# Two transformer layers on one core: layer 1's fill, tables and tail in another order

## The chip, the cores and the metric

The kernel runs on one core of one Trainium2 chip. The metric is the device time of one execution in microseconds; the time of a kernel is the median of its runs. Every number of the profile comes from one further execution, taken by the hardware profiler.

## The reference

Two layers work on x of shape (8, 256, 128), 8 batches of 256 tokens. Each layer first makes six vectors per batch from a condition, then an attention step and a feed-forward step. Cut to what matters:

```python
sa, ca, ga, sb, cb, gb = split6(silu(c) @ wmod)     # ga, gb kept at |.| >= 0.25
h = layernorm(x) * (1 + ca) + sa
x = x + ga * attention(h)                           # causal; layer 0: 16 heads of 8, layer 1: 16 heads of 64
h = layernorm(x) * (1 + cb) + sb
x = x + gb * ffn(h)
# ffn of layer 0: a shared gelu MLP, and top 2 of 8 experts
# ffn of layer 1: h + shared MLP + top 2 of 16 experts, by a sigmoid router;
#                 an MLP is (silu(h @ wg) * (h @ wu)) @ wd with 64 hidden values
```

All values are float32.

## The kernel before, in words

**Tiles and order.** Tokens stand 128 to a tile; four tiles, two batches, are a block of 512 columns, and there are four blocks (NW = 4, LAST = 3). The order of instructions is written by hand: each engine executes what is issued to it in program order, and it waits where an operand or a buffer isn't ready. Buffers come from pools; a tile takes a slot of its tag, and waits for the tile that had it before, so two uses of one tag with two slots can wait for each other. In PSUM the tags are `s` (two slots of two banks: scores, projections' hidden products `gu`, `gud`, `gus`), `o` and `sum` (one each), and `p` (two slots: what `ps_ln` hands out, the norm's transposes `nt1b`, the turned rows `xT`, the router's logits, the output product `y`).

**Layer 1's attention** runs over 32 units n (b, u = divmod(n, 4): batch and four heads). In unit n PE makes the scores of n (L1670), projects queries and keys for n+2 (L1639), values for n−1 (L1692, the output `o`; L1700, the sums) and projects values for n+2 (L1652); ACT takes exponentials (L1673), POOL masks the causal half (L822), DVE copies `o` out (L1704). Around each unit lists of further steps are hung in: `at(n)` before the values, `at_end(n)` after the unit, `at_head(n, k)` behind the k-th piece of scores. When the four units of a batch are done, `reciprocals1` (L1708 to L1716) takes the reciprocal of the sums, writes it to DRAM (`rd`) and reads it back spread over partitions (`rb`); `normalise1` (L1725) multiplies with it on DVE, and `finish1` (L1745 to L1752) is the output product on PE and the addition to x. For the last batch `spread_last` (L1733, L1737) spreads the reciprocals by a product on PE instead.

**Layer 1's feed-forward step, batches 0 to 5** (blocks 0 to 2) is sorted by expert. `norm1` makes the norm of a span of batches: `xn1b` (L766 on DVE), its transposes and h, the tokens `ht` (L1768, L1769 on POOL), and `add_h` (L1773, L1774 on POOL), which adds gb·h to x. `route1` (L1794 to L1820) picks the two experts and scatters the tokens into sorted rows `xs` in DRAM by indirect DMAs of POOL (L932). Before the first scatter `xs` is filled with zeros by `clear` (L889, one DMA of 12,582,912 bytes on SP's queue, issued at the end of unit 8). Then ten groups of four tiles of sorted rows are worked off: groups 0 to 3 are the first tiles of the 16 experts, in known places (`fetch_rows1`, L1830); groups 4 to 9 are the tiles that are needed beyond those, and which expert and which rows these are stands in two small tables, `rowi` and `widx`. `tables_steps` (L957 to L1004) makes them from the counts of tokens: a product on PE (L963) and 14 operations on DVE. SP reads the tables into registers, for the weights in `fetch_weights1` (L1850, L1854) and for the rows in `find_rows1`, and then loads with them (`load_rows`, L1046). Per group: `turn1` turns the rows (PE L1869, copied by ACT, L1871) and orders the rows of the group four further on, `hidden1` makes the two hidden products (PE L1880, silu on ACT L1885, multiplication on DVE L1886), `project_tiles` projects down (PE L1893) into two PSUM tiles, both copied by DVE (L1899) and stored (`ys`, L1900). When all is stored, 24 indirect DMAs of POOL (`gather1`, L1058) fetch each token's two rows, and `combine1` (PE L2018) adds them with weights, by products with diagonal matrices that `weigh1` makes on ACT (L2010).

**Batches 6 and 7** (block 3, LAST) are done densely, over all 16 experts, two at a time: `dense_hidden(p)` for p = 0 to 7 (PE L1942, silu on ACT L1936, multiplication on DVE L1937), `dense_gate(p)` (DVE L1947, the multiplication with the router's gates, which `gate_rows`, L1917 to L1927, spreads over partitions through DRAM) and `dense_project(p)` (PE L1952). `shared_hidden` and `shared_project` (L1962, L1976) are the shared MLP, and `ffn1_add` (L1988 to L1994) the last addition and the store of a block. The order of the tail stands as a plain list of calls at the end of the function.

**Layer 0** is in the change with one step: `gates0`, four small DVE operations (L1255 to L1259) that pick the gates, hung into an attention unit.

## Time and profile before

| what | us |
|---|---|
| runs of the kernel | 573.43, 575.76, 576.96 (median 575.76) |
| the profiled execution | 605.03 |
| its span (first to last instruction) | 603.2 |
| PE busy in the span | 543.5 (90%) |
| DVE busy | 323.8 (54%) |
| ACT busy | 265.5 (44%) |
| POOL busy | 265.2 (44%) |

The span begins at 0. A line of the timeline gives the start, the time from the first to the last of the instructions merged in it, engine, line of the kernel, operation, output and input tiles, their shapes, and how many instructions it holds; in brackets stand the idle time of the engine before it and what ended that. `PEld` is the loading of weights into PE, `SPq` the queue on which SP issues its DMAs. Where the releaser is "issue" or "remote", the trace shows nothing that the engine waited for. A line of the windows gives a stretch's start and end, its length, and each engine's busy time in it with the number of instructions; `PEclk` is the share of PE's full clock that was granted, 0.965 over the whole span.

### The profile page before, as it was taken

How to read it: one execution, taken by the hardware profiler on the slowest of the kernel's cores; microseconds unless marked ns; L12 is line 12 of the kernel's file. 1: busy time of each engine (PE TensorE's matmuls, PEld its weight loads, DVE VectorE, ACT ScalarE, POOL GpSimd, SP SyncE). 2: the span in 40 equal slices, each digit the busy share in tenths (PEclk: the TensorE clock that was granted, in tenths of full speed). 3: DMA queues.
4: the chain of work that ended last, by engine and by line, in shares of the span. 5: the costliest groups of instructions: out<-in, count | busy, mean ns of one | idle time of the engine just before them, and what ended most of it. 6: DMA issues, size and time to landing. Idle time of an engine off the chain costs nothing.

```text
span 603.2 us, 12004 instructions
## 1 busy us (share of the span) xinstructions
PE 543.5 (90%) x4499; PEld 384.4 (64%) x4499; DVE 323.8 (54%) x988; ACT 265.5 (44%) x495; POOL 265.2 (44%) x404
## 2 busy tenths in 40 slices
PE   5999998889999998999999989999999989885194
PEld 4355554468999986666767666766767677742064
DVE  4258886666422224655366646558374757771143
ACT  3678775244556633653344423462534322262010
POOL 5224576574444123855123525333563440647400
PEclk9999999799999999999999999999999999987688
DMA  8699100315999713104069831203030355555101
GB/s 278 243 399 406 56 19 27 129 44 155 327 342 354 238 39 153 36 18 99 1 211 408 326 72 46 60 3 71 14 93 10 82 175 170 166 148 131 36 19 57
DMA packets 53566, 85.40 MB, mean 142 GB/s; under 512 B 6652, under 2 KB 32764, under 8 KB 52348
## 3 DMA queue, kind: packets, MB, share of 16 engines
q1 hardware_dynamic: 45308, 60.50, 31.3%
q0 software_dynamic: 8048, 23.67, 12.1%
q8 instruction: 37, 0.61, 0.4%
q10 hardware_dynamic: 144, 0.39, 0.2%
q14 instruction: 29, 0.24, 0.1%
HBM read 53.46 MB, written 31.07 MB: 140 GB/s over the span
## 4 chain that ended last, share of the span: by engine, by line
PE 68%; DVE 12%; DMA 6%; ACT 5%; issue 3%; another core or an unknown queue 3%; SPq 1%; POOL 0%; DVEq 0%; ACTq 0%; POOLq 0%
PE sc L1670 6%; PE hp L1351 6%; PE yt L1359 6%; PE sc L1120 5%; PE o L1692 5%; PE qp L1639 5%; PE y L1745 5%; PE kp L1639 4%; PE vp L1652 4%; PE o L1154 3%; PE sum L1700 3%; DMA rb<-rd 2%; PE gud L1942 2%; DVE ou L1725 2%
## 5 line engine op out<-in xcount | busy, mean ns | idle before, releaser
L822 POOL TENSOR_SCALAR_AFFINE_SELECT pt<-pt 128x256 f32<-128x256 f32 (+1 forms) x144 | 67.1, 494 | 153.8 <-ACT pt L1673 118.3
L1058 POOL DMA_INDIRECT yg<-ys,yidx x56 | 53.9, 963 | 40.7 <-issue 20.5
L1673 ACT ACTIVATE pt<-sc 128x768 f32<-128x768 f32 x64 | 48.4, 808 | 31.2 <-PE sc L1670 31.1
L1136 ACT ACTIVATE pt<-sc 128x1024 f32<-128x1024 f32 x48 | 46.7, 1026 | 24.6 <-PE sc L1120 11.7
L1670 PEld LDWEIGHTS sc<-q,k 64*128 64x128 f32 x512 | 41.6, 187 | 18.7 <-issue 13.8
L1670 PE MATMUL sc<-q,k 64*128 64x256 f32 (+1 forms) x512 | 50.5, 337 | 0.0
L1353 ACT ACTIVATE hst<-hp,wt 128x128 f32<-128x128 f32 x136 | 38.8, 368 | 25.8 <-ACT hst L1353 24.2
L1692 PE MATMUL o<-pt,v 128*64 128x256 f32 (+1 forms) x512 | 48.7, 332 | 1.2 <-DVE ou L1704 1.2
L1655 ACT COPY v<-vp 128x512 f32<-128x512 f32 x32 | 18.7, 585 | 67.4 <-PE vp L1652 67.4
L1050 POOL DMA_INDIRECT wt<-in_wpk_dram,widx x31 | 29.5, 950 | 34.0 <-PE xT L1342 28.3
L1692 PEld LDWEIGHTS o<-pt,v 128*64 128x64 f32 x512 | 31.8, 136 | 18.2 <-issue 5.0
L1643 DVE COPY q<-qp 128x512 f32<-128x512 f32 x32 | 22.0, 688 | 37.3 <-PE qp L1639 37.3
L1364 DVE COPY ysb<-yt 128x128 f32<-128x128 f32 x39 | 11.3, 290 | 49.8 <-PE yt L1359 49.8
L1639 PE MATMUL qp<-h,wq 128*128 128x256 f32 x128 | 36.1, 404 | 1.7 <-DVE sh L1309 1.3
L1120 PE MATMUL sc<-qm,k 32*128 32x512 f32 x192 | 36.0, 722 | 1.4 <-ACT pt L1136 0.8
L1745 PE MATMUL y<-wo,ou 128*128 128x128 f32 x256 | 31.7, 281 | 5.9 <-DVE ou L1725 3.0
L932 POOL DMA_INDIRECT xs<-ht0b,idx x32 | 31.9, 998 | 11.2 <-issue 7.7
L1745 PEld LDWEIGHTS y<-wo,ou 128*128 128x128 f32 x256 | 29.9, 192 | 9.9 <-DVE at L922 4.6
L1652 PE MATMUL vp<-wv,h 128*128 128x512 f32 x64 | 36.0, 645 | 0.0
L1351 PE MATMUL hp<-xTs,wt 128*128 128x128 f32 x272 | 35.9, 275 | 0.0
L1359 PE MATMUL yt<-wt,hst 128*128 128x128 f32 x272 | 35.8, 275 | 0.0
L1351 PEld LDWEIGHTS hp<-xTs,wt 128*128 128x128 f32 x272 | 33.0, 192 | 0.0
(308 smaller groups left out, 1080.9 us busy)
## 6 DMA issues: line engine op xcount, KB each, us to landing
xs<-zero SPq DMA_DIRECT2D x1, 12288.0 KB
xs<-zero SPq DMA_DIRECT2D x1, 8192.0 KB
rb<-rd SPq DMA_DIRECT2D x14, 512.0 KB
mdb<-mrd SPq DMA_DIRECT2D x2, 2048.0 KB
xg<-xs SPq DMA_DIRECT2D x63, 64.0 KB
wt<-in_wpk_dram SPq DMA_DIRECT2D x24, 128.0 KB
wst<-in_wpk_dram SPq DMA_DIRECT2D x5, 514.0 KB
ys<-ysb SPq DMA_DIRECT2D x10, 256.0 KB
```

The source lines that it names most:

```text
L822: nc.gpsimd.affine_select(out=pt, in_=pt, compare_op=ALU.is_ge, fill=0.0, base=0, pattern=[[0, pt.shape[1]], [1, P]], channel_multiplier=-1,)
L1058: nc.gpsimd.indirect_dma_start(out=yg[:, k, :], out_offset=None, in_=self.ys[:, :], in_offset=bass.IndirectOffsetOnAxis(ap=self.yidx[:, j, ...
L1120: nc.tensor.matmul(out=sc[:, n, :].rearrange("p (a q) -> p a q", q=rhs.shape[2]), lhsT=k[r, cols], rhs=rhs, start=True, stop=u < 2,)
L1136: nc.scalar.activation(pt[:, bass.ts(half, 2), :], sc, AF.Exp)
L1351: nc.tensor.matmul(out=hp[:, c, :], lhsT=wt[:, bass.ts(c, P)], rhs=xT, start=True, stop=True)
L1359: nc.tensor.matmul(out=y, lhsT=hs[:, c, :], rhs=wt[:, bass.ds(WF + c * P, P)], start=(c == 0), stop=(c == FC - 1))
L1639: nc.tensor.matmul(out=ps_[:, n, :], lhsT=w1[f"w{what}1"][:, bass.ts(2 * u + n, P)], rhs=hb, start=True, stop=True)
L1652: nc.tensor.matmul(out=vp, lhsT=hb[:, bass.ts(j, P)], rhs=w1["wv1"][:, bass.ts(half, 512)], start=True, stop=True)
L1670: nc.tensor.matmul(out=sc[:, n, cols], lhsT=k[r, m, bass.ts(kb, P)], rhs=q[r, m, qs], start=True, stop=True)
L1673: nc.scalar.activation(pt, sc[:, :, 0:384], AF.Exp, scale=1.0 / math.sqrt(D1))
L1692: nc.tensor.matmul(out=o[bass.ts(n, D1), m, qs], lhsT=v[:, kb, bass.ts(4 * (u % 2) + 2 * m + n, D1)], rhs=pts[m][:, n, cols], start=(kb == ...
L1745: nc.tensor.matmul(out=y[:, j, :], lhsT=aT[:, c % 2, c // 2, bass.ts(j, P)], rhs=w1["wo1"][:, c, :], start=(c == 0), stop=(c == NC1 - 1),)
```

## The change

1. The fill of layer 1's `xs` is split into three DMAs of a third each, at the ends of units 4, 8 and 12, each behind the issues of that batch's reciprocals. The scatters wait for all three.
2. Layer 0's third step of the first gates goes from the end of unit 20 to the end of unit 21.
3. `spread_last` takes its PSUM tile from `ps_ln` (tag `p`) in place of tag `s`.
4. Of `project_tiles`' two copies out of PSUM the second goes from DVE to ACT.
5. `add_h` of the spans (2, 2) and (4, 1) comes one unit later (end of unit 23 and 27 in place of 22 and 26).
6. The first step of the tables and the weights of groups 4 and 5 go from the end of unit 29 to the end of unit 31, the tables ahead of what is done there already; the rows of groups 0 to 3 stay at unit 30 and so come ahead of the weights on SP's queue; the reading of the row table and the weights of group 6 go to the end of unit 31.
7. In the tail combines 0 to 3 go ahead of the dense gates, and hidden products, gates and dense products alternate: hidden(n), gate(n−2), product(n−2).

```diff
-        def clear(self, zero):
+        def clear(self, zero, part=0, parts=1):
             m = zero.shape[1]
-            self.fill = nc.sync.dma_start(
-                out=self.xs.rearrange("(p a) c -> p (a c)", p=P).rearrange("p (n m) -> p n m", m=m),
-                in_=zero.unsqueeze(1).to_broadcast([P, self.ne * self.cap // m, m]),
-            ).ins
+            n = self.ne * self.cap // m // parts
+            rows = self.xs.rearrange("(p a) c -> p (a c)", p=P).rearrange("p (n m) -> p n m", m=m)
+            self.fills.append(
+                nc.sync.dma_start(
+                    out=rows[:, bass.ts(part, n), :], in_=zero.unsqueeze(1).to_broadcast([P, n, m])
+                ).ins
+            )
...
-                tc.add_manual_dep(ins, self.fill.name, WAIT, reason="rows are cleared first")
+                for fill in self.fills:
+                    tc.add_manual_dep(ins, fill.name, WAIT, reason="rows are cleared first")
...
-    at_end(20, first_gates)
+    at_end(21, first_gates)
...
-            rp = pp.tile([P, 2, S], F32, tag="s", name=f"rp1_{u}")
+            rp = ps_ln([P, 2, S], f"rp1_{u}")
...
-        for k in range(2):
-            nc.vector.tensor_copy(ysb[:, :, k, :], y[k])
+        nc.vector.tensor_copy(ysb[:, :, 0, :], y[0])
+        nc.scalar.copy(ysb[:, :, 1, :], y[1])
...
-            at_end(n + 4 if bs[0] else n + 7, add)
+            at_end(n + 5 if bs[0] else n + 7, add)
     tables = one(z1.tables_steps(ps_ln, True))
-    at_end(29, tables, lambda: fetch_weights1(4), lambda: fetch_weights1(5))
-    at_end(30, *[lambda m=m: fetch_rows1(m) for m in range(4)], *[lambda m=m: find_rows1(m) for m in range(4, NQ)],
-          lambda: fetch_weights1(6))
+    at_end(30, *[lambda m=m: fetch_rows1(m) for m in range(4)])
+    ends[N - 1].insert(0, tables)
+    at_end(
+        N - 1, lambda: fetch_weights1(4), lambda: fetch_weights1(5),
+        *[lambda m=m: find_rows1(m) for m in range(4, NQ)], lambda: fetch_weights1(6),
+    )
...
-            if b == 2:
-                z1.clear(zero1)
+            if b < 4:
+                z1.clear(zero1, b - 1, 3)
...
     dense_hidden(2)
     dense_hidden(3)
+    combine1(0, 1, 2, 3)
     dense_gate(0)
-    dense_hidden(4)
     dense_gate(1)
-    dense_hidden(5)
-    dense_gate(2)
-    combine1(0, 1, 2, 3)
-    ffn1_add(0)
-    dense_hidden(6)
-    dense_gate(3)
     dense_project(0)
     dense_project(1)
+    dense_hidden(4)
+    dense_gate(2)
+    ffn1_add(0)
+    dense_project(2)
+    dense_hidden(5)
+    dense_gate(3)
+    dense_project(3)
+    dense_hidden(6)
+    dense_gate(4)
+    dense_project(4)
     dense_hidden(7)
-    dense_gate(4)
-    combine1(4)
-    dense_project(2)
     dense_gate(5)
-    dense_project(3)
-    combine1(5)
+    dense_project(5)
+    combine1(4, 5)
     dense_gate(6)
-    dense_project(4)
+    dense_project(6)
     combine1(6, 7)
     dense_gate(7)
     ffn1_add(1)
-    dense_project(5)
-    combine1(8)
-    dense_project(6)
-    combine1(9)
     dense_project(7)
-    combine1(10, 11)
     ffn1_add(LAST)
+    combine1(8, 9, 10, 11)
     ffn1_add(2)
```

More of the change, by code (lines that the diff above doesn't have):

```diff
@@ L867, in __init__ @@
             self.placed = 0
-            self.scatters = []
+            self.fills, self.scatters = [], []
             f32 = lambda shape, name: pool.tile(shape, F32, name=f"{name}{tag}")
```

## The prediction, made before the changed kernel had run

> **What bounds the kernel now.** I read the time in stretches first, to see which engine is full where, then the order of instructions around each place the diff touches. The windows (start and length, then each engine's busy time, the granted clock, the DMA share):

> ```profile
> core 0: us, PE busy (x) PEld busy (x) DVE busy (x) ACT busy (x) POOL busy (x), PEclk, DMA share, GB/s
> 300.00:400.00 100.00, 96.67 (x817) 67.69 (x814) 58.04 (x153) 42.12 (x60) 40.47 (x66) 1.00 0.51 170
> 540.00:560.00 20.00, 12.64 (x36) 5.40 (x34) 4.07 (x13) 3.52 (x10) 15.12 (x17) 0.76 0.62 136
> 560.00:575.00 15.00, 2.86 (x4) 1.30 (x5) 1.89 (x3) 1.08 (x2) 4.86 (x6) 0.61 0.11 28
> 575.00:603.00 28.00, 19.49 (x126) 15.34 (x124) 12.53 (x21) 2.39 (x4) 0.00 (x0) 0.87 0.11 40
> ```

> In layer 1's attention PE is busy 97 of 100 us: there only PE's own waits can be won. From 540 on it is not full, so there the order decides. The timeline of the end:

> ```profile
> 570.77 1.08 ACT L1936 ACTIVATE a<-gud 128x512 f32<-128x512 f32 x2 [14.93 <-remote]
> ...
> 581.03 1.02 PE L1942 MATMUL gud<-h,wu 128*128 128x512 f32 x2
> 582.09 0.60 ACT L1936 ACTIVATE a<-gud 128x512 f32<-128x512 f32 x1 [2.91 <-PE gud L1942]
> 582.72 0.69 DVE L1937 TENSOR_TENSOR a<-a,gud 128x512 f32<-128x512 f32 x1 [0.89 <-ACT a L1936]
> 583.32 0.68 DVE L1947 TENSOR_TENSOR a<-a,gp 128x512 f32<-128x512 f32 x1
> ```

> ACT stood 14.93 us before a silu whose input was ready, and 8.41 us before an earlier one (546.84 to 555.25), together 23.3 us, with no releaser in the trace. The profiled execution took 605.03 us (span 603.2) and the median of the runs is 575.76, 29.3 less. The attention is full of PE work and can't give 27 us back; if those two waits are away, PE's work from 542.5 is 8 hidden of 1.72 (13.8), one shared product 1.0, 8 dense products of 0.9 (7.3) and 12 combines of 0.44 (5.3), 27.4 us, to 570, and add and store bring the span to about 574.6, which with the 1.83 us around the span is 576.4. So I read the two waits as the profiled execution's own, and make every sum as a difference on its rows, carried over to 575.76. The 24 gathers (1.25 us apart from 536.60, last landing 567.9) would end at 572.1: PE's tail leads by only 2.5 us.

> **The change, part by part.** *Fill.* Now it is one 12.6 MB DMA from 306.63 to about 344.8. Behind it, the reciprocals' write of batch 2 takes 6.1 us (338.91 to 345.0), where the same write takes 1.7 at 303.72 and at 472.21; the broadcast lands at 352.46, and PE waits:

> ```profile
> 352.48 2.50 DVE L1725 TENSOR_TENSOR ou<-ou,rb 128x512 f32<-128x512 f32 x4 [5.06 <-DMA rb<-rd]
> 353.32 2.87 PE L1745 MATMUL y<-wo,ou 128*128 128x128 f32 x20 [2.25 <-DVE ou L1725]
> ```

> In thirds (10.3 us each, a batch apart, each behind the next broadcast) the write is 4.4 us earlier, and 1.9 of the 2.25 go (1.0 to 2.2): **−1.9**. The last third ends near 358, and the first scatter was at 360.31 and may be 2 earlier: POOL may wait up to 1.5, in front of the causal masks, which have 3 us of cover (they cost 1 if that is gone). The two added issues of 0.5 on SP lie between loads that nobody waits for: 0.

> *Added h a unit later.* DVE's four normalisations take 2.50 alone and 4.72 beside POOL's two additions, and at the second place (449.20) 3.99:

> ```profile
> 415.10 4.72 DVE L1725 TENSOR_TENSOR ou<-ou,rb 128x512 f32<-128x512 f32 x4
> 415.12 1.28 POOL L1773 TENSOR_TENSOR xn1b<-ht,mdb 128x512 f32<-128x512 f32 x1
> 416.47 1.60 POOL L1774 TENSOR_TENSOR x<-x,xn1b 128x512 f32<-128x512 f32 x1
> ...
> 420.01 3.84 PE L1745 MATMUL y<-wo,ou 128*128 128x128 f32 x32 [1.25 <-DVE at L922]
> ```

> PE waits 1.25 there and 1.70 at 453.35; about 2.4 of these 2.95 go. But one unit later the additions meet the normalisation L766 (two of 345 ns, at 429.75 and 463.16), and PE's transposes stand behind it, everything else of PE behind them. The nearest row is L766 beside a POOL operation at 249.84: 994 ns instead of 345, so 0.65 for one operation, about 0.9 a place with the second. [...] I take the row: **−0.6** (−2.4 to 0).

> *Layer 0's gates* (four DVE operations, 0.8 us) leave a place where PE waits 0.99 (103.02) and are put where it waits 0.38 (105.91): **0**. The clock is at half from 103.17 to 113.41 after a window 52% busy; if that is avoided, up to −3; if DVE is late at the new place, +0.5.

> *Tables, weights, rows.* SP's queue, in order of time:

> ```profile
> 484.97 5.38 SPq L1854 DMA_DIRECT2D wt<-in_wpk_dram  x8
> 490.66 2.05 SPq L1830 DMA_DIRECT2D xg<-xs  x4
> 495.37 1.96 SPq L1854 DMA_DIRECT2D wt<-in_wpk_dram  x4
> 497.58 6.75 SPq L1046 DMA_DIRECT2D xg<-xs  x12
> ```

> Today the table's 14 DVE operations (479.31 to 484.42) hold up a copy for which PE waits 1.15 at 485.17. That wait goes. But the table now waits for unit 31's work: its count can run at 486.4, and 4.85 us on, at 491.5, SP may read the indices. Then on SP, in order, 8 weight issues (0.52 each and one pause, 5.4 as above), seven register loads (2.35) and 4 more (2.0), 9.8 to 10.0; only then the four pieces of group 4's rows, issued 501.6 to 503.2 (before: to 499.45), landing 505 to 506 by the 2.5 they take now. The rows of groups 0 to 3 come earlier than before, and nobody waits for them. PE transposes group 4 at 501.34, ending 502.33; it would be at that place at 500.2 and wait 5, ending at about 505.9: **+3.6** (+2.5 to +5; behind it on PE stand hidden1(3) and all that follows, and nothing else is free to run). The clock: [...] it fell after windows 52% (99.75 to 103.17) and 56% busy (529.83 to 533.25), and not after one of 49% (523.01 to 526.42). [...] By the rows it falls for 3.4 us or more: cost up to 2. I take **+1.0**. Weights of groups 4 to 6 are loaded 6 to 7 us later and are wanted after their rows: covered while the rows are the later.

> *Reciprocals' spread in other buffers.* It leaves the pair shared with the hidden products (a wait of 1.31 at 513.44) for the pair of the norm's transposes, which then wait for DVE's multiplication of 0.7: **0** (−0.5 to +0.5).

> *Copies on two engines.* The tail where it matters:

> ```profile
> 531.08 4.79 ACT L2010 ACTIVATE dg<-ident,g 128x128 f32<-128x128 f32 x16
> 531.16 0.41 DVE L1899 COPY ysb<-yq_sum 128x256 f32<-128x256 f32 x1
> 531.29 0.49 PE L1893 MATMUL yq_o<-wt,aq 64*128 64x128 f32 x2 [1.25 <-DVE ysb L1899]
> ```

> Each of ten groups has 0.41 less on DVE, and ACT pays 0.38 each (its silu of the same shape). PE waits for these copies only in groups 7 to 9: about −0.6. But in ACT's program order eight diagonals (half of 4.79, 2.4) stand ahead of group 8's copy, which so ends at 533.4; PE's last group, which needs that buffer, ends at 534.1 instead of 532.3, the gathers start 1.45 later, and the first shared silu at 538.3 instead of 537.18. Net **+0.8** (0.3 to 1.5).

> *Dense products by turns.* In the new order PE does hidden(n), then the product n−2, which needs gate n−2. On DVE gate n−2 stands behind the multiplication of n, that behind the silu of n, and that behind hidden(n) itself. So after each of n = 4, 5, 6, 7 PE has nothing between the end of hidden(n) and the end of that gate. From the rows at 581: hidden ends 582.05, silu 582.09 to 582.69, multiplication to 583.41, gate to 584.00: 2.0 us. Before, products and combines of older groups lay in this gap. 4 × 2.0 = **+8.0**. Gate 0, moved ahead, may wait for the gates' spread: **+0.5** (0 to 1.5). At the end combines 8 to 11 lie beside the last additions: **−0.5**.

> Sum: −1.9 − 0.6 + 0 + 3.6 + 1.0 + 0 + 0.8 + 8.0 + 0.5 − 0.5 = **+10.9**. On the profiled execution as it stands 605.03 would become 616; on the median 575.76 it is **586.7 us**.

> **The rivals.** *The waits of ACT are real in every run, or the gathers hide the turns.* Then combines 0 to 3 and products 0 and 1 (3.7 us of PE work), which now stand ahead of hidden(4), fall into the wait, and the gathers' own chain hides part of the turns: the last stretch costs +2.5 instead of +8.0, and the time is 581. For it: the trace does show the waits. Against it: 27 us fit nowhere else. *The clock falls in the turns.* A turn is 1.72 + 0.98 of work in 4.7, 57% busy, like the windows after which it fell; at half clock over two of the four turns, 2 × 2.7 more: 592; over all of them 597. *Faster:* one mechanism, the place of PE in the trace when group 4's rows land. If these land by 502 (SP not waiting for the table, say 4 us earlier than I have it), the 3.6 and 1.0 are a gain of 1.15, and without that hole the clock keeps up in the tail; with the turns inside ACT's waits (0) and the clock at 103 whole (−3), the sum is −1.9 − 0.6 − 1.15 − 3 = −6.7: 569. It decides at a landing before 502.3. Against it, the table can't start before unit 31's sums. *Nothing:* the gains in the attention and losses behind it cancel, 576; it needs the turns to cost under 3.

> **How the numbers follow.** A difference of 1% (5.8 us) is about what a measurement of this kernel can tell. Forecast 586.7: 0.42; turns half hidden, 581: 0.17; clock falls, 592 to 597: 0.14; nothing, 573 to 579: 0.12; faster, 569: 0.15. The third of these lies wholly above 1%, the first nearly so, of the second a third lies within: slower 0.66, same 0.18, faster 0.16. The range 570 to 596 leaves out the faster half of the last case and the far end of the clock's.

> **What would show it.** Right: no wait of PE at the output product of batch 2; L1725 all near 0.63 us, and L766 slower once or twice; a wait of 4 to 5 us at group 4's transposes, put down to the row's DMA; group 9's products waiting for ACT's copy; and four gaps of 2 us of PE, each ahead of a dense product, with DVE's gate as releaser. Wrong: rows of group 4 there before PE, gaps under 1 us, or ACT's long waits again in the unprofiled time.

## The result, and the profile after

The changed kernel takes 592.35 us (median of 587.9 to 596.18, four runs), the kernel before 574.6 (571.46 to 576.96): 1.031 times as long, 95% interval 1.022 to 1.040. Run once more beside its parts (experiment 5) it took 593.53 against 575.8, 1.034 (1.027 to 1.041). So it is slower by some 18 us, in the stated range; the forecast of 586.7 had +10.9. The profile after is that of the longest of the four runs: 596.18, 593.0, 591.7 and 587.9 us went with mean granted clocks of 0.966, 0.971, 0.973 and 0.975.

On the chip of experiments 1 to 4 the kernel before itself takes 605.64 us (43 runs), and ACT's long waits in the tail are there in every trace (the longest 12.82 to 17.76 us); on the two chips of 5 to 8 and of 9 to 12 it takes 575.8 and 574.96, and they are in none. So each kernel is compared by its ratio to before on its own chip. The ratios of experiments 5 to 8 stand against the 38 of before's 59 runs there that lie below 576.08 us (median 574.21); by the medians of all runs they are 1.0308, 0.9939, 1.0033 and 1.0009.

The windows of the tail after, with the columns as before (start and end, length, busy time of each engine, clock, DMA share, GB/s):

```profile
540.00:560.00 20.00, 15.89 (x72) 9.01 (x70) 7.55 (x18) 5.20 (x13) 15.22 (x16) 0.91 0.63 135
560.00:575.00 15.00, 10.73 (x34) 5.37 (x35) 4.07 (x7) 1.19 (x2) 4.77 (x5) 0.76 0.16 44
575.00:594.50 19.50, 9.27 (x60) 6.98 (x58) 6.69 (x12) 0.60 (x1) 0.00 (x0) 0.76 0.12 44
```

Behind 560 no engine is near full, PE included, and the clock is at 0.76. One turn of the new order in the timeline (lines have moved by 4: L1946 is the hidden product, L1940 the silu, L1941 the multiplication, L1951 the gate, L1956 the dense product):

```profile
567.82 1.87 PE L1946 MATMUL gud<-h,wg 128*128 128x512 f32 x2
569.49 1.91 PE L1946 MATMUL gud<-h,wu 128*128 128x512 f32 x2
571.44 0.60 ACT L1940 ACTIVATE a<-gud 128x512 f32<-128x512 f32 x1 [5.99 <-PE gud L1946]
572.07 0.69 DVE L1941 TENSOR_TENSOR a<-a,gud 128x512 f32<-128x512 f32 x1 [5.30 <-ACT a L1940]
572.67 0.68 DVE L1951 TENSOR_TENSOR a<-a,gp 128x512 f32<-128x512 f32 x1
573.41 1.16 PE L1956 MATMUL of<-wd,a 128*128 128x128 f32 x8 [2.01 <-DVE a L1951]
```

The chain is the one forecast: hidden, silu, multiplication, gate, and PE idle for 2.01 us until the gate is done. It is there four times (560.25, 566.83, 573.41, 579.76), 2.01 each. But the hidden product takes 3.6 us (567.82 to 571.40) where it took 1.9 in the profile before (580.17 to 582.05): a turn lasts 6.58, not 4.7. The windows of PE's clock, cut where the clock changes, show at which clock it ran:

```profile
550.79:554.20 3.41, 1.46 (x13) 1.00 0.85 172
554.20:557.61 3.41, 3.41 (x9) 0.50 0.25 61
557.61:561.02 3.41, 1.40 (x8) 1.00 0.22 60
561.02:564.44 3.42, 3.42 (x8) 0.50 0.45 129
564.44:567.85 3.41, 1.40 (x10) 1.00 0.18 46
567.85:571.26 3.41, 3.41 (x6) 0.50 0.00 0
571.26:574.68 3.42, 1.41 (x10) 1.00 0.00 0
```

In these rows each stretch of 3.41 us with a gap in it has PE busy for 1.40 to 1.46, 41 to 43%, and the next is granted 0.50; there PE is busy for 3.41, the clock of the one behind it is 1.00, and the next gap lies in that. The turn at this mixture of clocks, 6.58, is nearly two stretches (6.83), and the two alternate from 550.79 to 578.09.

Group 4's rows and the copies, in the timeline after:

```profile
483.16 2.05 SPq L1834 DMA_DIRECT2D xg<-xs  x4
487.08 8.92 SPq L1858 DMA_DIRECT2D wt<-in_wpk_dram  x12
496.25 6.12 SPq L1050 DMA_DIRECT2D xg<-xs  x12
...
498.42 1.20 PE L1873 MATMUL xT<-ident,xg 128*128 128x128 f32 x3 [4.59 <-DMA xg<-xs]
...
531.18 0.58 PE L1897 MATMUL yq_sum<-wt,aq 64*128 64x128 f32 x1 [2.43 <-ACT ysb L1903]
```

PE waits 4.59 us for the rows of group 4, and 2.43 for ACT's copy ahead of group 9, both as forecast. And the new place of the added h:

```profile
422.75 1.27 POOL L1777 TENSOR_TENSOR xn1b<-ht,mdb 128x512 f32<-128x512 f32 x1
422.90 2.55 DVE L766 TENSOR_SCALAR xn1b<-x,mv1b,rstd1b 128x128 f32<-128x128 f32 x2
424.10 1.26 POOL L1778 TENSOR_TENSOR x<-x,xn1b 128x512 f32<-128x512 f32 x1
425.50 0.33 PE L775 MATMUL nt1b<-ident,xn1b 128*128 128x128 f32 x1 [0.94 <-DVE xn1b L766]
```

Two operations of DVE, 0.60 us together in the profile before, take 2.55 beside POOL's two.

### The profile page after: what moved, and what is told of

Read it like the earlier page. It is cut to its first block, busy times and chain, and to the rows that moved or that the text cites. A ratio compares the mean times of both kernels' runs of the same rounds, so it can differ in the third digit from the quotient of the medians.

```text
span 594.5 us, 12006 instructions
## 1 busy us (share of the span) xinstructions
PE 544.1 (92%) x4499; PEld 383.2 (64%) x4499; DVE 322.1 (54%) x978; ACT 269.3 (45%) x505; POOL 264.2 (44%) x404
## 5 line engine op out<-in xcount | busy, mean ns | idle before, releaser
L1363 PEld LDWEIGHTS yt<-wt,hst 128*128 128x128 f32 x272 | 33.0, 192 | 0.0
```

The source lines that it names most:

```text
L1363: nc.tensor.matmul(out=y, lhsT=hs[:, c, :], rhs=wt[:, bass.ds(WF + c * P, P)], start=(c == 0), stop=(c == FC - 1))
```

## The experiments

In the order of running; 1 to 4 ran on one chip, 5 to 8 on a second, 9 to 12 on a third. The theory is that the turns cost PE four gaps of 2 us, and the clock besides; the rival, that the loss is spread over the parts, late rows and copies above all. "By all runs" means the ratio of the medians of all runs, as above.

**1. Gates first in the turns** (on the chip of 605.64). PE's order is that of the changed kernel; only DVE's differs.

```diff
-    dense_hidden(4)
-    dense_gate(2)
+    dense_gate(2)
+    dense_hidden(4)
...
```

> The changed kernel with one kind of line swapped: gate n-2 is issued ahead of hidden(n), n = 4 to 7, so that on DVE it no longer stands behind the multiplication of n; PE's order is the same. Theory (PE waits for a gate that DVE makes late, and the clock falls because of these waits): the four gaps of 2.0 us and the half clock behind them go, 8.0 + 7.4 = 15.4 us less than the changed kernel's 592.4, so about 577, 1.005 of before. Rival (the turns are slow for another reason, the gathers or the clock by itself): no change, 592. Rival (gaps alone, the clock stays at half): 584.

Measured 609.03, 1.0051 (1.0029 to 1.0074): the ratio of the theory. But the trace shows ACT's waits, among them

```profile
576.75 1.09 ACT L1940 ACTIVATE a<-gud 128x512 f32<-128x512 f32 x2 [17.76 <-remote]
```

in which work of the tail may be hidden, so it is run again as 9.

**2. The gaps filled with useless products** (same chip). Behind hidden(n) PE makes two products into the buffer that hidden(n+1) then overwrites.

```diff
     dense_hidden(4)
+    dense_warm(5)
     dense_gate(2)
...
```

> The changed kernel with two useless products of 128x512 on PE in each of the four gaps; they are overwritten, so the output is the same. The gaps' 2.0 us stay, but PE is busy in them (1.7 of 2.0). Theory (about half of the loss in the turns is the clock, 4 x 1.86 us): the turns take 4.7 us in place of 6.58, so 592.4 - 7.4 = 585, 1.018 of before. Rival (the clock has fallen for what happened before the turns, and the filling does not bring it back): 592 or more, up to 4 x 1.7 more where the useless products run at half clock, 596.

Measured 616.9, 1.0181 (1.0139 to 1.0222); the value of the theory as a ratio, but without the changed kernel beside it on this chip. Run again as 10.

**3. The changed kernel with the tail of before** (same chip): the whole tail list of before in place of the new.

```diff
-    combine1(0, 1, 2, 3)
-    dense_gate(0)
+    dense_gate(0)
+    dense_hidden(4)
...
```

> The changed kernel with the tail's order of before; the other six edits stay. Theory (the tail's order is the loss, the rest is small: fill -1.9, added h -0.6, gates 0 to -2, rows of group 4 +2.7 and clock +1, copies +0.8): 574.6 + 0 to +3, so 575 to 578, 1.00 to 1.005 of before. Rival (the later rows of group 4 and the copies carry a third of the loss or more): 580 to 582, 1.01 and more.

Measured 608.37, 1.0046 (1.0024 to 1.0068). The six other edits together cost half a per cent, so the tail should be the loss; the changed kernel itself was not run on this chip.

**4. The new tail alone** (same chip): the kernel before with the list of the changed kernel.

```diff
+    combine1(0, 1, 2, 3)
     dense_gate(0)
-    dense_hidden(4)
...
```

> The kernel before with the new order of the tail alone. Theory: the whole loss, 4 x 2.0 of gaps, 1.95 for the wait of product 0 for the gates' spread less what the old order lost itself, 7.4 by the clock: 590 to 592, 1.027 to 1.031 of before. Rival (the losses are spread over the parts): 583 to 586.

Measured 614.36, 1.0138 (1.0094 to 1.0182). Neither: it lies just under the rival's 583 to 586 (1.0146 to 1.0198) and far from the theory's 1.027. Either the losses are spread, or the waits of this chip hide half of the new tail's loss. Experiment 11 tells them apart.

**5. The changed kernel again** (from here on before takes 575). No edit.

> The changed kernel once more, on the chip that also runs its parts. Theory (the turns cost 8 us of gaps and 7 of clock whatever ACT does before them): 1.027 to 1.035 of before on a chip where before takes 575; where before takes 605, with ACT's long waits in every run, the 3.7 us of combines and products that are moved ahead fall into those waits and the ratio is 1.015 to 1.025. Rival (the waits of ACT hide nothing): 1.03 on any chip.

Measured 593.53, 1.0337 (1.0269 to 1.0406).

**6. The three edits in the attention alone**: the fill in thirds, the added h and layer 0's gates.

```diff
+            if b < 4:
+                z1.clear(zero1, b - 1, 3)
...
+            at_end(n + 5 if bs[0] else n + 7, add)
...
+    at_end(21, first_gates)
```

> The kernel before with the fill in thirds, added h one unit later and layer 0's gates one unit later; nothing else. Theory (these three are gains, as the trace of the changed kernel has it 4.8 us ahead of before at the last reciprocals): 3 to 5 us less, 0.992 to 0.995 of before. Rival (the lead at that point came from a shifted clock window and not from the edits): 1 to 2.5 less, 0.996 to 0.998.

Measured 572.29, 0.9960 (0.9935 to 0.9985): 2.3 us less, and 3.5 less by all runs (0.9939). The first is the rival's value, the second the theory's, so the total does not decide. The traces tell more. From the reciprocals' write of batch 0 to that of batch 6 the nine traces with the fill in thirds and the later added h take 195.3 to 197.6 us, the five without them 198.6 to 200.9: these edits are gains. But of the 4.8 us that the profile after is ahead, 2.4 were there before either of them acts; half clock in layer 0 lasted 10.24 us in the profile before and 6.83 in the one after.

This trace also shows how the old order of the tail ends where ACT does not wait:

```profile
564.03 1.01 PE L2022 MATMUL of<-yg,dg 128*128 128x128 f32 x4 [0.56 <-DMA yg<-ys,yidx]
```

PE waits for the last gather, here and in 7, 8 and 12 (0.35 to 0.61 us): PE's work and the gathers end almost together. In the traces of the new order (5, 9, 10, 11) no such wait stands at the end.

**7. The tables' place alone.**

```diff
-    at_end(29, tables, lambda: fetch_weights1(4), lambda: fetch_weights1(5))
+    at_end(30, *[lambda m=m: fetch_rows1(m) for m in range(4)])
+    ends[N - 1].insert(0, tables)
...
```

> The kernel before with the tables and the weights of groups 4 to 6 moved to the end of the attention; nothing else. Theory (group 4's rows come 3 to 4 us late, the copy's wait of 1.15 goes, the clock falls after the 5 us wait): +2.5 to +5, 1.005 to 1.009 of before. Rival (the gathers or ACT's waits behind it hide the delay): 0 to +1, 1.000 to 1.002.

Measured 577.68, 1.0050 (1.0020 to 1.0081): +2.9 us, the lower end of the theory; by all runs +1.9 (1.0033), between it and the rival.

**8. The copies alone.**

```diff
-        for k in range(2):
-            nc.vector.tensor_copy(ysb[:, :, k, :], y[k])
+        nc.vector.tensor_copy(ysb[:, :, 0, :], y[0])
+        nc.scalar.copy(ysb[:, :, 1, :], y[1])
```

> The kernel before with the second copy out of PSUM on ACT; nothing else. Theory (eight diagonals stand ahead of group 8's copy on ACT, and the gathers start 1.4 us later): +0.3 to +1.5, 1.0005 to 1.003 of before. Rival (shorter copies on DVE are what counts): -0.6, 0.999.

Measured 576.33, 1.0043 (1.0019 to 1.0068): a loss of 2.5 us, but of 0.5 by all runs (1.0009). So a price is likely and its size is not settled; 0.3 to 1.5 was expected.

**9. Gates first, again.** The edit of 1.

> The changed kernel with gates ahead of the hidden products once more, to have it beside the changed kernel's 593 on a chip where before takes 575. Theory: gaps and half clock of the turns both go, 15 us less than 593, 576 to 580, 1.002 to 1.009 of before. Rival (on this chip something else fills the turns): 590 or more.

Measured 580.35, 1.0094 (1.0064 to 1.0124), against 1.0337 for the changed kernel. In the trace, one of the shorter of thirteen runs (576.11 us, clock 0.982 where the thirteen have 0.964 to 0.983), the turns are packed, at full clock throughout:

```profile
557.07 1.05 PE L1956 MATMUL of<-wd,a 128*128 128x128 f32 x8
557.27 0.60 ACT L1940 ACTIVATE a<-gud 128x512 f32<-128x512 f32 x1 [3.01 <-PE gud L1946]
557.90 0.69 DVE L1941 TENSOR_TENSOR a<-a,gud 128x512 f32<-128x512 f32 x1 [2.32 <-ACT a L1940]
557.96 1.02 PE L1946 MATMUL gud<-h,wg 128*128 128x512 f32 x2
558.51 0.68 DVE L1951 TENSOR_TENSOR a<-a,gp 128x512 f32<-128x512 f32 x1
```

Here the dense product runs before the multiplication of the same turn has even begun. Of what is left, 1.0094 against 1.0053 for the other parts added up (2.4 us), 1.8 are three waits of PE of 0.81, 0.73 and 0.23 for gates.

**10. The gaps filled, again.** The edit of 2.

> The changed kernel with the four gaps filled by useless products, once more beside 575. Theory: the gaps stay and the clock does not fall, so 7 us less than 593, 584 to 588, 1.016 to 1.022 of before. Rival (the clock was not the cause of the turns' length, only their companion): 592 to 596.

Measured 585.55, 1.0185 (1.0141 to 1.0230). One turn (L1957 hidden, L1948 useless products, L1962 the gate, L1967 the dense product):

```profile
563.34 1.88 PE L1948 MATMUL gud<-h,wg 128*128 128x512 f32 x4
563.54 0.60 ACT L1940 ACTIVATE a<-gud 128x512 f32<-128x512 f32 x1 [4.29 <-PE gud L1957]
564.17 0.69 DVE L1941 TENSOR_TENSOR a<-a,gud 128x512 f32<-128x512 f32 x1 [3.60 <-ACT a L1940]
564.77 0.68 DVE L1962 TENSOR_TENSOR a<-a,gp 128x512 f32<-128x512 f32 x1
565.51 1.16 PE L1967 MATMUL of<-wd,a 128*128 128x128 f32 x8 [0.30 <-DVE a L1962]
```

The gate comes no earlier, PE only works in the meantime for nothing, and a turn takes 4.89 at a clock of 1.00. So more work on PE makes the kernel faster (585.55 for 593.53): here the half clock is a cost of its own, and it is gone when the gaps are filled. From the start of hidden(4) to the end of product 5 PE takes 25.64 us in the changed kernel (555.12 to 580.76), 19.56 here (551.84 to 571.40) and 11.44 with the gates first (549.13 to 560.57): 8.1 for the gaps, 6.1 for the clock. In the trace of experiment 5 the same stretch takes 25.61.

**11. The new tail alone, again.** The edit of 4.

> The kernel before with the new order of the tail alone, once more beside 575. Theory: the turns carry 14 to 16 of the change's 17.7 us, 589 to 592, 1.024 to 1.028 of before. Rival (the parts add up to more than the sum, the clock falls in the turns only because group 4's rows came late before): 582 to 585, 1.013 to 1.016.

Measured 590.09, 1.0273 (1.0235 to 1.0310), +15.7 us: the tail is the loss, and the intervals of 4 and 11 lie apart. On the chip where ACT waits in the tail anyway, about half of it is hidden, as the first rival of the prediction had it for every run. But the trace of 4 has the four gaps of 2.01 us as well (582.30 to 599.84), so what is hidden there lies ahead of the turns, and not in them. The windows of the clock here:

```profile
551.92:555.33 3.41, 1.76 (x5) 1.00 0.21 58
555.33:558.75 3.42, 2.88 (x12) 1.00 0.35 119
558.75:562.16 3.41, 1.58 (x10) 1.00 0.28 63
562.16:565.58 3.42, 1.41 (x5) 1.00 0.20 58
565.58:568.99 3.41, 3.41 (x11) 0.50 0.00 0
```

The first turns are slow by their gaps only: stretches of 1.76 and 1.58 busy have 1.00 behind them. Then one holds 1.41, and the next is granted 0.50.

The kept traces give the tail's price as a whole. From the end of group 9's products to the last instruction the old order takes 43.5 to 43.9 us (6, 7, 8, 12), the new one 57.6 here and 62.1 and 62.2 in the two traces of the changed kernel, 53.1 with the gaps filled and 46.5 with the gates first.

**12. The fill and the added h, nothing else.**

```diff
+            if b < 4:
+                z1.clear(zero1, b - 1, 3)
...
+            at_end(n + 5 if bs[0] else n + 7, add)
```

> The kernel before with the two edits that won waits of PE, the fill in thirds and added h one unit later; layer 0's gates, tables, copies and the tail as before. Theory (the gates' move costs about 1 us: in all traces that have it PE waits 2.26 for h there, without it 0.4 to 1.4): 1 us better than with the gates, 0.990 to 0.996 of before. Rival (the gates' place does not matter): 0.996, as with it.

Measured 570.58, 0.9930 (0.9906 to 0.9954): faster than both kernels, by 4.0 us against before. Against 6, which has layer 0's gates moved as well, it is 0.3% less, but the intervals overlap: whether the gates cost anything is not settled. (In the traces of 6 and 12 the wait of PE for h in layer 0 is 2.26 with the move and 1.38 without.)

## Why the prediction was right, and where its sizes were off

The direction and the place were right. The parts, each run alone where before takes 575, add up: attention −0.40%, tables +0.50%, copies +0.43%, tail +2.73%, together +3.26%; the whole is +3.37% (2.69 to 4.06). By all runs the first three are −0.61, +0.33 and +0.09, the sum 2.5% and the whole 3.1%, which leaves 0.5% open, within the interval of the whole. The spread of the reciprocals was not run alone; it has no more room than that.

| step | forecast, us | measured, us |
|---|---|---|
| fill, added h, gates | −1.9, −0.6, 0: −2.5 | −2.3 (−3.7 to −0.9), by all runs −3.5; experiment 6 |
| tables, and the clock behind | +3.6, +1.0: +4.6 | +2.9 (+1.2 to +4.7), by all runs +1.9; experiment 7 |
| copies | +0.8 | +2.5 (+1.1 to +3.9), by all runs +0.5; experiment 8 |
| tail: turns, gate 0, end | +8.0, +0.5, −0.5: +8.0 | +15.7 (+13.5 to +17.8), experiment 11 |

*Dense products by turns.* "4 × 2.0" was exact: 2.01 four times, 8.1 between experiments 9 and 10. The term that failed is the one that was left out of the likeliest sum and put among the rivals with 0.14: the clock. The measured 592.35 is that rival's figure, so the stated range held because it took the rival in. The clock costs 6.1 in the trace of the changed kernel (25.64 − 19.56), and 2.2 in that of experiment 11 (21.77 for the same stretch), where one stretch of the turns was at half clock. The forecast had the evidence, 57% busy per turn, but judged the mean over a turn. In the profile after the clock fell behind single stretches, in which, with the gap inside, PE has 1.40 to 1.46 of 3.41 us of work, 41 to 43%. The 6.1 is about the price of two of four turns at half clock, as the rival had it (2 × 2.7).

*Gate 0 and the end.* PE waited 1.95 and 1.40 for gate 0 in the two traces of the changed kernel and 0.81 to 0.91 in experiments 9 to 11, where 0.5 (0 to 1.5) was forecast. DVE's first gate is released by the landing of the gates' spread (`gp`), after a wait of 1.64 us in the profile after, 0.49 in experiment 9 and 0.59 in 11. With the gates first and the clock full in the turns, the new tail is still 2.7 us longer than the old one (46.5 against 43.5 to 43.9), where +0.5 and −0.5 had been set: a second term that was too small.

*Tables.* SP's queue ran as written out: rows ahead of twelve weights, group 4's rows issued from 496.25 where 501.6 less the 4.8 of lead gives 496.8. PE waited 4.59 for the forecast 5. After the wait the clock was at half from 496.17 to 503.00, 6.8 us, where the forecast's +1.0 assumed 3.4 or more; the stretch before had PE busy for 1.07 of 3.41.

*Copies.* The wait was at the forecast place (2.43 us for ACT's copy, behind eight diagonals), and from the start of group 9's transposes to the end of its last product the traces with the edit take 10.0 to 10.6 us, without it 7.7 to 8.3 (9.1 with the tables moved, 9.5 in experiment 4). That is some 2 us, where 1.8 was forecast (534.1 for 532.3), ahead of the stores that the gathers wait for; how much of it reaches the whole time is open, as said under 8.

*Fill.* The wait of 2.25 at the output product of batch 2 is gone, and between the reciprocals' writes of batches 2 and 3 the nine traces with the fill in thirds take 30.0 to 30.7 us, the five without it 33.2 to 35.6 (2.5 less or more; 1.9 forecast). The longest is experiment 11's. The first scatter then waited 2.61 for the last third at 357.43, beyond the 1.5 allowed for it; the masks had the cover, and no wait of PE follows.

*Added h.* Here the step took too small a number, the nearest row (994 ns beside POOL): the first L766 took 1.22 us and the second 1.41, in place of 0.35, and each ends 0.1 us behind a POOL operation (422.75 + 1.27 and 424.10 + 1.26). The second is recorded as starting 0.06 us ahead of the POOL operation that it outlasts, and what lengthens the two is not shown. PE's two waits at this place are 0.54 and 0.94, at the second place 0.40: 1.9 lost in all, by chance the same as the 1.8 that was forecast. Of the 2.95 us at the old places 1.84 came back (the wait at 447.80 is still 1.11), so the move is worth about nothing in this trace. From the write of batch 3 to that of batch 6, where it acts, the traces take 100.1 to 102.1 us with it and 100.1 to 102.7 without. So most of what 6 and 12 win should be the fill's; neither edit was run alone.

*The base of the sum.* "The two waits of ACT are the profiled execution's own" fell. On the chip of 605 they are in all four traces; on the others in none of the eight. The difference of 29.3 was right, its cause not: it goes with the chip, not with profiling. Whether it belongs to the chip or to a condition that lasted through those runs is not shown. What holds ACT there is open too: in experiment 1 the silus at 576.75 come 17.76 us after ACT's last work although PE's products for them are recorded as done by 563.55, the trace names no releaser, and no experiment took that apart. The other reading of the base, that PE's tail leads the gathers by 2.5 us, came out as a tie: without ACT's waits PE waits 0.35 to 0.61 for the last gather in the old order, so the gathers can hide next to nothing of the turns.

## What to carry to other kernels

When an order "by turns" puts a product two steps behind its hidden layer, look at the queue of the engine that makes its last operand: the step there must be issued ahead of the work that needs the newest result, or the distance of two is a distance of none; issuing the four gates one step earlier took back some 13 us. A gap of PE in a tail like this one is to be priced twice: here it cost its length (2.0 us) and, where the clock fell, the half clock of the stretch behind it (6.1 us over four turns in one trace, 2.2 in another). The mean busy share of a turn, 57% in the forecast, did not tell that: the stretches of the turns behind which the clock fell in the profile after, the gap inside, were 41 to 43% busy. And several edits in one change hide each other: the fill with the added h was 0.7% faster within a change that lost 3%.

## What was not expected of the hardware

```profile
550.57:553.98 3.41, 1.61 (x13) 1.00 0.94 180
553.98:557.40 3.42, 3.42 (x12) 0.50 0.17 47
```

- Useless products on PE made the kernel faster: 1.0185 with them against 1.0337 (1.0308 by all runs) without.
- The same kernel takes 605.64 us on one chip and 575.8 and 574.96 on two others, and an edit's price differs with it: the new tail 1.0138 on the one, 1.0273 on the other.
